# Local attention in float32 parts: the scores' second product from one part of the queries, two heads in the two halves of the array's rows

## The chip, the cores and the metric

The kernel runs on one core of a Trainium2 chip, as one launch. TensorE (PE) multiplies matrices and writes its results to PSUM, which has eight banks of 512 float32 numbers for each of 128 partitions; ScalarE (ACT), VectorE (DVE) and GpSimd (POOL) do the rest; SyncE (SP) issues most of the transfers. The metric is the device time of one execution in microseconds. Three runs of the kernel before took 5764.69, 5766.54 and 5771.52 us; the median is 5766.54 us.

## The reference

The input x is 4 sequences of 2048 tokens with 256 features, in float32. The reference does two things one after the other.

1. A layer norm, then full self-attention with 16 heads of 16 features and a Gaussian prior on the distance added to the scores, an output projection, and the sum with x.
2. A layer norm, then two layers of a local transformer. This is the part that the change touches. Each layer shifts half of the features by one token, projects to queries, keys and values of 8 heads of 64 features, brings queries and keys to unit length, scales and rotates them, and lets each block of 128 queries look at the keys of its own block and of the block before:

```
sim = einsum('bhwid,bhwjd->bhwij', bq, bk)        # 128 queries x 256 keys, 64 features
sim = where((i < j) | (i > j + 128) | (j == -1), -max, sim)
out = einsum('bhwij,bhwjd->bhwid', softmax(sim), bv)
```

After the output projection and the sum comes a second layer norm and a gated unit (256 to 2 x 682, GELU, back to 256).

## The kernel before

The first attention and the preparation of the layers' weights come first (`attention`, up to about 3120 us of the span). Its order is written out by hand. The change does not touch it, but its matmuls are rows to measure with: L859 and L942 are products over 64 rows of the array, written `64*128` in the profile (64 active rows, 128 active columns), two of them side by side; L966 uses the array in quarters of its columns (`128*32`).

The layers are in `local_layers`. A step is one block of 128 tokens of one sequence in one layer: 2 layers x 4 sequences x 16 blocks = 128 steps, and each fourth step also begins the gated unit for four blocks. The pieces of a step are entered in a timetable (`AT`, `put`): 32 slots for a step, with later steps interleaved, so that a step's pieces lie between those of its neighbours. A slot is a place in program order, not a time. From that order a planner makes the order of each engine's instructions at compile time, with its own costs for what is ready when; so a piece can be cut, and others put between its parts.

Products are made accurate by parts: a float32 operand is a high part, rounded to the fast matmul type (fp32r), and a low part, the rest. `dense` (L404) multiplies high by high, high by low and low by high.

For the scores, `attend` does the following:

- `turn` (L1458) transposes queries and keys, two heads to a block of 128 rows: a pair of heads has parity 0 in rows 0 to 63 and parity 1 in rows 64 to 127.
- `high_q` (L1463, ScalarE) and `low_q` (through `low`, L1356, VectorE) fill the queries' tile `lq`. For each parity the high part lies in the head's own 64 rows and the low part in the other 64.
- `high_k` (L1472, ScalarE) and `low_k` (L1356, VectorE) make the keys' two parts in the head's own rows of `lk`, and two transfers (L1478, issued by SyncE) copy both parts to the other 64 rows. The tile has two slots, for the block's own keys and those before.
- `product` (L1494, "sim") then multiplies over all 128 rows: the stacked queries (high over low) with the high keys, twice over, and with the low keys, twice over. That is four terms in two matmuls for each head, 16 matmuls in a step, each 256 columns wide (128 at the first block of a sequence). A pair of heads takes one PSUM bank; the four pairs are at slots 54, 59, 62 and 59.
- `masked` (L1506, VectorE) adds the mask, writes the scores to SBUF and takes their maximum; `weights` (L1520, ScalarE) makes the exponentials; `normalize` (L1531, POOL) divides by the sums.

`gather` of the same step follows: `turn_p` (L1553, "pT") transposes the weights, `copied` (L1564, ScalarE and VectorE by turns) takes them out of PSUM, and `weigh` (L1574, "po") multiplies them with the values, with the array in halves of its columns (`128*64`). The PSUM banks of all of these, of the gated unit's products (`w<-gt,ww`, `w<-ww,mid`) and of the output product `lo` come from one pool of six; the projections `qkv` have two of their own. When a bank's readers are done, another tile can have it.

Of the kernel before, what the change touches and what calls it, by code (L numbers as in the profile page):

```python
# [28 lines left out]
F32 = mybir.dt.float32  # L29
# [8 lines left out]
P = 128  # L38
# [55 lines left out]
    "unit": (22, 15, 41),  # L94
    "turn": (36, 41),
    "parts": (51, 52, 44, 44),
    "sim": (54, 59, 62, 59),
    "masked": (59, 59, 63, 63),
    "weights": (59, 61, 69, 70),
    "normalize": (73, 77, 75, 77),  # L100
# [87 lines left out]
def encoder_kernel(  # L188
# [22 lines left out]
    nc = tc.nc  # L211
# [1072 lines left out]
    def local_layers():  # L1284
        with ExitStack() as es:
# [11 lines left out]
            def psum(name):  # L1297

                banks = pq if name.startswith("qkv_") else pp
                return banks.tile([P, 512], F32, tag="ps", name=name)  # L1300

            qst = [fp.tile([P, 2, 4, P], F32R, tag=f"q{i}", name=f"lq{i}") for i in range(2)]
            kst = fp.tile([P, 2, 2, 2, 4, P], F32R, tag="k", name="lk")
            own = (slice(0, LD), slice(LD, P))
# [16 lines left out]
            def put(at, key, pieces):  # L1324

                assert len(pieces) == len(AT[key]), key
                for slot, piece in zip(AT[key], pieces):
                    tt.put(at + slot, piece)

            def each(f, n):  # L1330
                return [partial(f, i) for i in range(n)]
# [22 lines left out]
            def low(dst, src, h):  # L1354

                nc.vector.tensor_tensor(dst, src, h.bitcast(F32), ALU.subtract)  # L1356
# [88 lines left out]
            def attend(at, l, b, c):  # L1445

                name = f"{l}_{b}_{c}"
                s = state[l, b, c]
                m = {}
                q, slot = qst[c % 2], c % 2  # L1450
                k = kst[:, :, :, slot]

                def turn(i):
                    flat = s["r"][:, i].rearrange("p h d -> p (h d)")
                    ps = psum(f"{'qk'[i]}t_{name}")
                    for pair in range(4):
                        cols = slice(pair * P, (pair + 1) * P)
                        nc.tensor.transpose(ps[:, cols], flat[:, cols], ident)  # L1458
                    m["t", i] = ps.rearrange("p (a t) -> p a t", a=4)

                def high_q():
                    for par in range(2):
                        nc.scalar.copy(q[own[par], par], m["t", 0][own[par]])  # L1463

                def low_q():
                    for par in range(2):
                        r, other = own[par], own[1 - par]
                        low(q[other, par], m["t", 0][r], q[r, par])

                def high_k():  # L1470
                    for par in range(2):
                        nc.scalar.copy(k[own[par], par, 0], m["t", 1][own[par]])  # L1472

                def low_k():
                    for par in range(2):
                        r, other = own[par], own[1 - par]
                        low(k[r, par, 1], m["t", 1][r], k[r, par, 0])
                        nc.sync.dma_start(k[other, par].bitcast(F32), k[r, par].bitcast(F32))  # L1478

                put(at, "turn", each(turn, 2))  # L1480
                put(at, "parts", [high_q, low_q, high_k, low_k])


                width = 2 * P if c else P
                windows = slice(0, 2 if c else 1)
                masks = mask[:, P * (1 - slot) : P * (1 - slot) + width]

                def product(pair):
                    ps = m["ps", pair] = psum(f"sim_{name}_{pair}").rearrange(
                        "p (a t) -> p a t", a=2  # L1490
                    )
                    for par in range(2):
                        for part in range(2):
                            nc.tensor.matmul(  # L1494
                                ps[:, par, :width], q[:, par, pair, :],
                                kst[:, par, part, windows, pair, :], start=part == 0, stop=part == 1,
                            )

                def masked(pair):
                    if pair == 0:  # L1500
                        s["p"] = wp.tile([P, LH, 2 * P], F32, tag="sim", name=f"sim_{name}")
                        for key in ("top", "sums", "inv"):
                            m[key] = small.tile([P, LH], F32, tag=f"l{key}", name=f"{key}_{name}")
                    for par in range(2):
                        h = 2 * pair + par
                        nc.vector.tensor_tensor_reduce(  # L1506
                            s["p"][:, h, :width], m["ps", pair][:, par, :width], masks, 1.0,
                            3.0 * MASKED, ALU.add, ALU.max, m["top"][:, h : h + 1],
                        )
                    if pair % 2:  # L1510
                        hs = slice(2 * pair - 2, 2 * pair + 2)
                        nc.vector.scalar_tensor_tensor(  # L1512
                            m["top"][:, hs], m["top"][:, hs], -1.0, s["rn"][:, hs],
                            ALU.mult, ALU.mult,
                        )

                def weights(pair):
                    for h in (2 * pair, 2 * pair + 1):
                        w = s["p"][:, h, :width]
                        nc.scalar.activation(  # L1520
                            w, w, AF.Exp, bias=m["top"][:, h : h + 1],
                            scale=s["rn"][:, h : h + 1], accum_out=m["sums"][:, h : h + 1],
                        )

                def normalize(pair):
                    if pair % 2 == 0:
                        hs = slice(2 * pair, 2 * pair + 4)
                        nc.vector.reciprocal(m["inv"][:, hs], m["sums"][:, hs])  # L1528
                    hs = slice(2 * pair, 2 * pair + 2)
                    w = s["p"][:, hs, :width]  # L1530
                    nc.gpsimd.tensor_tensor(  # L1531
                        w, w, m["inv"][:, hs].unsqueeze(2).to_broadcast([P, 2, width]), ALU.mult
                    )

                put(at, "sim", each(product, 4))
                put(at, "masked", each(masked, 4))
                put(at, "weights", each(weights, 4))
                put(at, "normalize", each(normalize, 4))
# [244 lines left out]
            for step, (l, b, c) in enumerate(steps):  # L1783
                at = SLOTS * (step + 1)
                if b == 0 and c == 0:
                    if l:
                        tt.put(at + AT["spread"][0], partial(load, l, ("q", "k", "v")))
                    tt.put(at + AT["turn"][0], partial(load, l, ("wo",)))
                    tt.put(at + AT["stats"][0] - 20, partial(load, l, ("w1", "w2")))
                if c % 4 == 0:  # L1790
                    tt.put(max(0, at + FETCH_AT), partial(fetch, l, b, c // 4))
                project(at, l, b, c)
                attend(at, l, b, c)
                gather(at, l, b, c)
                if c % 4 == 0:
                    glu(at, l, b, c // 4)
            tt.run()

    attention()
    local_layers()  # L1800


# [51 lines left out]
```

## Time and profile before

| | before |
|---|---|
| median of three runs | 5766.54 us |
| profiled execution | 5772.22 us, span 5770.4 us |
| mean granted TensorE clock | 0.985 |
| sim matmuls, L1494 | 2048, 339.8 us busy, mean 295 ns |
| their weight loads | 2048, median 189 ns |
| copies of the keys, L1478 | 256 transfers of 256 KB |

Busy time is by instructions, and matmuls are pipelined: a matmul's length in the profile runs from its start to its modelled end, and the next may start long before that. So lengths of matmuls are not added up; the distance from one start to the next says what a matmul costs in a stream. PEld is the loading of weights, which runs beside the matmul before it. A row of the timeline gives the start, the length of the whole group, the engine, the line, the operation, the tiles (output <- inputs), the active rows * columns of the array for PE, the shape, the number of instructions, and in brackets the idle time of the engine just before with what ended it. An idle time of an engine that does not bound the kernel costs nothing.

### The profile page before, as it was taken

The numbers are of one execution on the slowest core, as the hardware profiler recorded it, in microseconds if no ns is written. First come the engines' busy times: TensorE is split into PE (matmuls) and PEld (weight loads), VectorE is DVE, ScalarE is ACT, GpSimd is POOL, SyncE is SP. The second block draws the span as 40 slices with busy tenths as digits, with TensorE's granted clock in tenths as the row PEclk, the third lists the DMA queues.
The fourth block names the chain that finished last, engine by engine and source line by source line (L and its number), as shares of the span: only waits on it lengthen the run. The fifth ranks groups of instructions, "written<-read, shape, count | busy, mean of one in ns | idle before, by whom it ended". The sixth has DMA issues, their size and how long they took to land.

```text
span 5770.4 us, 105485 instructions
## 1 busy us (share of the span) xinstructions
PE 5470.7 (95%) x35544; PEld 3390.2 (59%) x35544; DVE 4836.5 (84%) x13769; ACT 4465.9 (77%) x9400; POOL 2184.3 (38%) x2368
## 2 busy tenths in 40 slices
PE   7999999999999999999997999999999999999998
PEld 4444444444444444444444787888887888888787
DVE  6878999789998789999994888888888788888886
ACT  3879998789988799989996676666666666667665
POOL 3222112221022210010002565666665666666665
PEclk8999999999999999999998999999999999999999
DMA  4444233443234423332213112221223222222211
GB/s 153 140 123 123 79 94 99 124 129 102 84 111 131 130 78 103 87 96 59 67 49 110 51 48 55 51 55 52 55 51 84 83 61 58 60 60 55 67 51 40
DMA packets 337243, 477.30 MB, mean 83 GB/s; under 512 B 67297, under 2 KB 191201, under 8 KB 335169
## 3 DMA queue, kind: packets, MB, share of 16 engines
q1 hardware_dynamic: 323744, 434.36, 27.0%
q0 software_dynamic: 12960, 36.20, 2.2%
q8 instruction: 284, 4.65, 0.3%
q14 instruction: 255, 2.08, 0.1%
HBM read 267.80 MB, written 126.09 MB: 68 GB/s over the span
## 4 chain that ended last, share of the span: by engine, by line
PE 57%; DVE 22%; ACT 8%; POOL 6%; DMA 3%; issue 3%; SPq 0%; POOLq 0%; DVEq 0%; ACTq 0%
PE s L859 16%; PE acc L966 15%; PE s L942 8%; PE w L404 5%; ACT sim L1520 4%; PE sim L1494 3%; DVE s L873 3%; PE qkv L404 3%; POOL rn L373 3%; DVE lk L1356 2%; PE po L1574 2%; DVE sim L1506 2%; DVE hn L1639 2%; DVE tops L871 2%; PE pqk L404 1%
## 5 line engine op out<-in xcount | busy, mean ns | idle before, releaser
L957 ACT ACTIVATE e<-s 128x512 f32<-128x512 f32 x4096 | 2151.1, 612 | 230.9 <-PE s L942 125.4
L859 PE MATMUL s<-k,q 64*128 64x512 f32 x3200 | 1296.2, 466 | 103.0 <-DVE tops L873 69.0
L873 DVE CUSTOM_DVE_ANT_0 s<-s,wide 128x512 f32<-128x512 f32 x1408 | 976.8, 694 | 197.6 <-PE s L859 185.9
L966 PE MATMUL acc<-e,v 128*32 128x512 f32 x8192 | 1100.1, 609 | 0.3 <-ACT rest L980 0.3
L859 PEld LDWEIGHTS s<-k,q 64*128 64x128 f32 x3200 | 531.9, 185 | 550.0 <-ACT more L879 259.1
L942 PE MATMUL s<-q,k 64*128 64x512 f32 x4096 | 833.7, 418 | 5.2 <-issue 2.6
L1520 ACT ACTIVATE sim<-sim,top,rn 128x256 f32<-128x256 f32 (+1 forms) x1024 | 597.2, 586 | 257.5 <-DVE top L1512 256.9
L871 DVE TENSOR_REDUCE tops<-s 128x1 f32<-128x512 f32 x896 | 610.8, 682 | 76.2 <-PE s L859 72.7
L1531 POOL TENSOR_TENSOR sim<-sim,inv 128x512 f32<-128x512 f32 (+1 forms) x512 | 512.8, 1022 | 345.5 <-DVE inv L1528 345.4
L942 PEld LDWEIGHTS s<-q,k 64*128 64x128 f32 x4096 | 542.2, 186 | 130.6 <-ACT e L957 53.4
L883 DVE CUSTOM_DVE_ANT_0 more<-s,more 128x512 f32<-128x512 f32 x896 | 614.3, 686 | 0.3
L859 PEld LDWEIGHTS s<-kd,q 64*128 64x128 f32 x896 | 165.2, 184 | 748.6 <-DVE tops L873 384.3
L879 ACT ACTIVATE more<-s 128x512 f32<-128x512 f32 x896 | 539.7, 602 | 76.3 <-PE s L859 44.4
L404 PE MATMUL w<-gt,ww 128*128 128x512 f32 x2112 | 545.8, 397 | 3.5 <-DVE lk L1356 3.1
L953 DVE TENSOR_TENSOR s<-s,band 128x187 f32<-128x187 f32 (+2 forms) x1408 | 468.7, 354 | 60.5 <-PE s L942 59.8
L859 PE MATMUL s<-kd,q 64*128 64x512 f32 x896 | 447.7, 500 | 0.5 <-DVE tops L871 0.2
L404 PEld LDWEIGHTS w<-gt,ww 128*128 128x128 f32 x2112 | 387.5, 189 | 79.3 <-issue 3.7
L1506 DVE CUSTOM_DVE_ANT_0 sim<-sim,cst 128x256 f32<-128x256 f32 (+1 forms) x1024 | 376.9, 409 | 60.1 <-PE sim L1494 56.8
L1419 POOL TENSOR_TENSOR r<-r,t 128x256 f32<-128x256 f32 x512 | 366.7, 738 | 150.5 <-DVE t L1406 141.0
L997 POOL TENSOR_TENSOR oall<-o,inv 128x256 f32<-128x256 f32 x64 | 39.8, 621 | 983.8 <-DVE inv L996 982.2
L373 POOL TENSOR_TENSOR rn<-ss,nhalf 128x16 f32<-128x16 f32 x128 | 372.7, 2912 | 95.6 <-DVE ss L372 92.7
L1494 PE MATMUL sim<-lk,lq 128*128 128x256 f32 (+1 forms) x2048 | 339.8, 295 | 27.6 <-DVE lq L1356 18.8
(196 smaller groups left out, 9667.6 us busy)
## 6 DMA issues: line engine op xcount, KB each, us to landing
lk<-lk SPq DMA_DIRECT2D x256, 256.0 KB
k<-sm SPq DMA_DIRECT2D x512, 96.0 KB
q<-sm SPq DMA_DIRECT2D x508, 96.0 KB
sm<-part SPq DMA_DIRECT2D x168, 256.0 KB
q<-sm SPq DMA_DIRECT2D x128, 192.0 KB
k<-sm SPq DMA_DIRECT2D x126, 192.0 KB
fg<-f SPq DMA_DIRECT2D x32, 512.0 KB
tb<-td SPq DMA_DIRECT2D x128, 128.0 KB
```

The lines of the kernel that those rows point to most:

```text
L373: nc.gpsimd.tensor_tensor(dst, var, nhalf[:, : var.shape[1]], ALU.pow)
L404: nc.tensor.matmul(ps, a, c, start=first and k == 0 and i == 0, stop=last and k == n - 1 and i == 2,)
L859: nc.tensor.matmul(ps, q1[u // 4 % Q_BUFS][rows, u % 4 * P : (u % 4 + 1) * P], keys, start=True, stop=True,)
L871: nc.vector.tensor_reduce(top, ps, AX.X, ALU.max)
L873: nc.vector.tensor_tensor_reduce(ps, ps, prior, 1.0, LOWEST, ALU.add, ALU.max, top)
L879: nc.scalar.activation(more, pairs.pop((u, 1, half)), AF.Relu)
L883: nc.vector.tensor_tensor_reduce(more, ps, more, 1.0, LOWEST, ALU.add, ALU.max, tops[u // NC][:, chunk(u), 2 * half : 2 * half + 1],)
L942: nc.tensor.matmul(ps, k2[s // 4 % Q_BUFS][rows, kc % 4 * P : (kc % 4 + 1) * P], q2[h % 2][rows, j % 2 * QT : (j % 2 + 1) * QT], start=Tru ...
L957: nc.scalar.activation(e, sums.pop((s, j)), AF.Exp)
L966: nc.tensor.matmul(acc[32 * j : 32 * j + 32, :], vs[b, kc][:, own * VS : own * VS + 32], es_.pop((s, j)), start=kc == 0, stop=kc == NC - 1,)
L1494: nc.tensor.matmul(ps[:, par, :width], q[:, par, pair, :], kst[:, par, part, windows, pair, :], start=part == 0, stop=part == 1,)
L1520: nc.scalar.activation(w, w, AF.Exp, bias=m["top"][:, h : h + 1], scale=s["rn"][:, h : h + 1], accum_out=m["sums"][:, h : h + 1],)
```

## The change

The product with the keys' high parts stays as it is, over all 128 rows. The product with the keys' low parts takes the queries' high parts alone: both lie in the head's own 64 rows, so it is a matmul over 64 rows, and the heads of parity 0 and 1 use the upper and the lower half of the array. The term of low queries by low keys is left out. The low keys need no second copy, so the transfers copy the high keys alone (128 KB instead of 256), and they are issued before `low_k`'s subtractions, after `high_k`.

Two matmuls that run side by side in row halves write to different banks. So the bank is no longer that of a pair of heads but that of a parity: the pieces are two halves of four heads (two pairs), each with two banks, one for each parity, in which the two pairs lie side by side. Within a half come first the four full-array matmuls, then the four over 64 rows. The first matmul into a bank sets `start`, and the last sets `stop`. The halves are at slots 55 and 60. `masked` reads its pair's part of both banks.

```diff
--- before.py
+++ after.py
@@ -94,7 +94,7 @@
     "unit": (22, 15, 41),
     "turn": (36, 41),
     "parts": (51, 52, 44, 44),
-    "sim": (54, 59, 62, 59),
+    "sim": (55, 60),
     "masked": (59, 59, 63, 63),
     "weights": (59, 61, 69, 70),
     "normalize": (73, 77, 75, 77),
@@ -1302,6 +1302,7 @@
 
 
 
+
             qst = [fp.tile([P, 2, 4, P], F32R, tag=f"q{i}", name=f"lq{i}") for i in range(2)]
             kst = fp.tile([P, 2, 2, 2, 4, P], F32R, tag="k", name="lk")
             own = (slice(0, LD), slice(LD, P))
@@ -1474,8 +1475,12 @@
                 def low_k():
                     for par in range(2):
                         r, other = own[par], own[1 - par]
+                        nc.sync.dma_start(
+                            k[other, par, 0].bitcast(F32), k[r, par, 0].bitcast(F32)
+                        )
+                    for par in range(2):
+                        r = own[par]
                         low(k[r, par, 1], m["t", 1][r], k[r, par, 0])
-                        nc.sync.dma_start(k[other, par].bitcast(F32), k[r, par].bitcast(F32))
 
                 put(at, "turn", each(turn, 2))
                 put(at, "parts", [high_q, low_q, high_k, low_k])
@@ -1485,16 +1490,23 @@
                 windows = slice(0, 2 if c else 1)
                 masks = mask[:, P * (1 - slot) : P * (1 - slot) + width]
 
-                def product(pair):
-                    ps = m["ps", pair] = psum(f"sim_{name}_{pair}").rearrange(
-                        "p (a t) -> p a t", a=2
-                    )
-                    for par in range(2):
-                        for part in range(2):
-                            nc.tensor.matmul(
-                                ps[:, par, :width], q[:, par, pair, :],
-                                kst[:, par, part, windows, pair, :], start=part == 0, stop=part == 1,
-                            )
+                def product(half):
+                    banks = [
+                        psum(f"sim_{name}_{half}{par}").rearrange("p (a t) -> p a t", a=2)
+                        for par in range(2)
+                    ]
+                    for i in range(2):
+                        m["ps", 2 * half + i] = [ps[:, i, :width] for ps in banks]
+
+
+                    for part, rows in enumerate(((slice(0, P),) * 2, own)):
+                        for pair in (2 * half, 2 * half + 1):
+                            for par in range(2):
+                                nc.tensor.matmul(
+                                    m["ps", pair][par], q[rows[par], par, pair, :],
+                                    kst[rows[par], par, part, windows, pair, :],
+                                    start=part == pair % 2 == 0, stop=part == pair % 2 == 1,
+                                )
 
                 def masked(pair):
                     if pair == 0:
@@ -1504,7 +1516,7 @@
                     for par in range(2):
                         h = 2 * pair + par
                         nc.vector.tensor_tensor_reduce(
-                            s["p"][:, h, :width], m["ps", pair][:, par, :width], masks, 1.0,
+                            s["p"][:, h, :width], m["ps", pair][par], masks, 1.0,
                             3.0 * MASKED, ALU.add, ALU.max, m["top"][:, h : h + 1],
                         )
                     if pair % 2:
@@ -1532,7 +1544,7 @@
                         w, w, m["inv"][:, hs].unsqueeze(2).to_broadcast([P, 2, width]), ALU.mult
                     )
 
-                put(at, "sim", each(product, 4))
+                put(at, "sim", each(product, 2))
                 put(at, "masked", each(masked, 4))
                 put(at, "weights", each(weights, 4))
                 put(at, "normalize", each(normalize, 4))
```

## The prediction

> **What bounds the kernel now.** I read the page first (shares, slices, groups), then a table of busy time by stretch, then TensorE's timeline around the changed products, then the waits of those products.
>
> ```profile
> PE 5470.7 (95%) x35544; PEld 3390.2 (59%) x35544; DVE 4836.5 (84%) x13769; ACT 4465.9 (77%) x9400; POOL 2184.3 (38%) x2368
> L942 PE MATMUL s<-q,k 64*128 64x512 f32 x4096 | 833.7, 418 | 5.2 <-issue 2.6
> L1494 PE MATMUL sim<-lk,lq 128*128 128x256 f32 (+1 forms) x2048 | 339.8, 295 | 27.6 <-DVE lq L1356 18.8
> ```
>
> The table by stretch, for the two long steady stretches of the layers (columns: length, then busy time of PE, PEld, DVE, ACT, POOL, the granted clock, DMA):
>
> ```profile
> 3200.00:4400.00 1200.00, 1144.80 (x8148) 959.48 (x8148) 1008.08 (x2743) 826.38 (x1934) 740.96 (x674) 1.00 0.21 55
> 4460.00:5600.00 1140.00, 1087.86 (x7759) 915.78 (x7759) 953.55 (x2584) 784.50 (x1832) 744.16 (x667) 1.00 0.23 62
> ```
>
> TensorE is busy 95% in both stretches at full clock, VectorE 84%, so a nanosecond of TensorE there is nearly a nanosecond of the end. The layers run from about 3120 us to the end: 128 steps (2 layers, 4 batches, 16 blocks) of 20.2 us in the steady part. The attention ahead of them is not touched. L1494, the changed line, has 16 matmuls in each step.
>
> TensorE's timeline of one step (start, length, group):
>
> ```profile
> 4514.42 0.74 PE L1494 MATMUL sim<-lk,lq 128*128 128x256 f32 x4
> 4514.99 1.56 PE L404 MATMUL qkv<-wv,ht 128*128 128x512 f32 x6
> 4516.39 1.58 PE L404 MATMUL w<-ww,mid 128*128 128x256 f32 x12
> 4517.81 1.12 PE L1494 MATMUL sim<-lk,lq 128*128 128x256 f32 x8
> 4518.86 1.09 PE L1574 MATMUL po<-pT,lv 128*64 128x128 f32 x16
> 4519.88 1.70 PE L404 MATMUL w<-ww,mid 128*128 128x256 f32 x12
> 4521.42 0.64 PE L1494 MATMUL sim<-lk,lq 128*128 128x256 f32 x4
> 4521.90 1.55 PE L404 MATMUL qkv<-wq,ht 128*128 128x512 f32 x6
> ```
>
> Lengths overlap, so I read from start to start. Twelve matmuls of 256 columns take 4517.81 - 4516.39 = 1.42 us, 0.118 each; six of 512 take 1.40, 0.23 each. Now the changes of the array's shape. The 8 sim matmuls ahead of po (array in column halves, 128*64) take 1.05 us where 8 x 0.118 = 0.94: **leaving** a shape costs 0.09 to 0.11. The 12 w matmuls that follow po take 1.54, not 1.42: **entering** one costs 0.12, for the first matmul's weights have nothing to hide behind. Sim after po, in another step, shows it again: 0.58 for 4, where 4521.42 to 4521.90 is 0.48.
>
> ```profile
> 4500.12 0.74 PE L1494 MATMUL sim<-lk,lq 128*128 128x256 f32 x4
> 4500.70 1.53 PE L404 MATMUL qkv<-wq,ht 128*128 128x512 f32 x6
> ```
>
> Row halves (64*128), which the change uses, appear beside full-array work only early in the attention:
>
> ```profile
> 58.63 1.68 PE L404 MATMUL pv<-aw,xT 128*128 128x256 f32 x12
> 60.24 0.50 PE L859 MATMUL s<-kd,q 64*128 64x512 f32 x1
> ...
> 61.55 0.49 PE L859 MATMUL s<-k,q 64*128 64x512 f32 x1 [0.58 <-ACT more L879]
> 61.97 1.68 PE L404 MATMUL pv<-aw,xT 128*128 128x256 f32 x12
> ```
>
> The 12 full-array matmuls between them take 1.61 us: 1.42 + 0.10 + 0.09. And one lone half-row matmul takes 0.42 until the full array starts, against 0.23 in a stream: 0.19 for entering and leaving. So a change to or from row halves costs what one to column halves does, about **0.20 us** (0.19 to 0.22).
>
> **What the change removes.** Of the 16 matmuls of a step, the 8 with the keys' low parts now take 64 rows each, two side by side. The nearest row for that is L942: 418 ns each, yet 833.7 busy us over 4096, 0.204 each, half of the length, so pairs do overlap. Eight slots of 0.118 become four: **-0.47 us a step** (at block 0 of each sequence, 8 steps with 128 columns, -0.24 to -0.44).
>
> **What it adds.** Each group of 8 goes full array, row halves, and on. Half 0 needs a change in and a change out. Half 1 needs one in; its way out falls together with the change that sim (or w) makes before po already. So 3 more changes x 0.20 = **+0.60 us a step**; the return from po to full-array work is there before and after. Net +0.13 us in the ordinary step. In about one step of four (30) the first-layer product `w<-gt` of the gated unit stood between the sim matmuls and po, and there the change out is paid again: +0.33. Sum: 90 x 0.13 + 30 x 0.33 + 8 x 0.25 = 11.7 + 9.9 + 2.0 = **+24 us**. With 0.19 and 0.22 for a change instead: +19 and +32.
>
> The Trainium skill, "TensorE: Matmul & The Clock Gate", Part 3, gives the span of packed tiles as one matmul's length plus about 4 ns for each further tile and prices no change of shape; "TensorEngine Tiling (Array Packing)", Key Properties, says that changing the mode drains the array and gives no price. By the first alone, an estimate, the pairs would gain about 59 us. The rows above price the drain, so I go by the rows.
>
> **Cuts.** The layers' order is the planner's, which mixes pieces by its own costs; in this trace's timeline sim runs are cut at times (2 matmuls, then another product, then the rest). A cut inside a row-half block costs two more changes, 0.40. I estimate 15 cuts in 256 blocks: +6 us (bounds 0 and 20).
>
> **What moves.** SyncE's two key copies now wait for ScalarE's rounding alone, not for VectorE's subtractions (L1356, 0.69 us each), and carry half the bytes. SP's queue behind them (table loads, fetches, the shift copies) is released earlier by as much; those waits have slack and I cost them at nothing. If that cover were gone, they would still be earlier, not later. VectorE's low parts are the same two instructions. What the products wait for:
>
> ```profile
>   DVE lq L1356: 46.1, 57
>   DMA lk<-lk: 15.7, 20
> ```
>
> The copy's 15.7 us (PE's and PEld's idle together) shrinks: I take **-10** (bounds -15.7 and 0). The 46.1 for the queries' low parts: in the steady part one step of four stands some 0.9 us there, because the filling work had already been used up:
>
> ```profile
> 3412.98 0.96 PE L1494 MATMUL sim<-lk,lq 128*128 128x256 f32 x4 [0.65 <-DVE lq L1356]
> ```
>
> The full-array product still comes first and still needs those parts, so I leave it: 0 (bounds -46 and 0).
>
> **Banks.** Before, a pair of heads took one bank; now a half takes two at once and keeps them until both its pairs are masked. The total is the same, the pressure is not: six banks, of which two hold the second product's sums during nearly two steps of four. TensorE already waits for banks:
>
> ```profile
> PE pT L1553 <- DVE lk L1356: 31.2, 65, 1.5
> PE pT L1553 <- DVE lq L1356: 14.4, 28, 0.5
> ```
>
> A half that finds no second bank waits for one copy out, 0.68 us (L1564 on VectorE). Bounds: 0 and 64 x 0.68 = +44; less than nothing is possible only through the planner. I take +3, near the low end, for the planner can put other matmuls there. The masking (L1506) reads the same columns, 0.42 us each.
>
> **Sum.** 24 + 6 - 10 + 0 + 3 = +23 us. The profiled execution took 5772.2 us (span 5770.4), 5.7 above the median of the runs; against the median, 5766.5 + 23 = 5789.5, so **5790**.
>
> **Rivals.**
> 1. *Faster by a vanished wait.* Half 0 is placed a little later, behind the values' product (6 x 0.23 = 1.4 us), which covers both waits in front of sim, 61.8 us in all. Then 24 + 6 + 3 - 62 = -29: 5738. It ends faster once more than some 45 of the 62 us go. For: in the ordinary step the values' product does come right after sim. Against: where the 0.9 us are lost, another product had already been taken ahead (qkv of wk stood just before sim).
> 2. *Slower by banks.* +44 instead of +3: 5831. For: the waits of pT. Against: in the step shown, ScalarE had copied two of the four transposes out (4511.95 and 4514.27 + 0.58) before or just as sim began, so two banks were free.
> 3. *The change of shape is free*, -59 - 10: about 5698. Against: 0.42 against 0.23 above.
> 4. *The halves don't run side by side* (the change doesn't do what it says): +0.47 more in a step, +60: 5850. Against: L942's busy time.
>
> **How the numbers follow.** Forecast 0.52, its own range 5772 to 5812 (switch price, cuts and copy at their bounds); rival 1 0.20; rival 2 0.14; rival 3 0.03; rival 4 0.03; 0.08 for a planner's order that evens it out. A difference within 0.2% (11.5 us, about what a measurement of this kernel can tell from none) gets those 0.08, 0.04 of the forecast's low end and 0.03 of rival 1: 0.15. Faster: 0.17 + 0.03 = 0.20. Slower: the rest, 0.65. The range 5740 to 5834 leaves out rivals 3 and 4, and the outer parts of 1 and 2: about 0.2.
>
> **What would show it.** Right: sim rows in two forms, 128*128 and 64*128, 8 matmuls a step of each; in each half about 0.21 us from the last full-array start to the first pair, 0.22 to 0.24 from the first pair to the second, 0.21 to what follows; a group of 8 takes 0.99 to 1.05 us where 0.94 was; steps 0.1 to 0.3 us longer; copies of 128 KB. Wrong: a start-to-start of 0.12 across a change of shape (rival 3), sim without waits and steps under 20.2 us (rival 1), new idle time ahead of sim ended by VectorE's copies or masks (rival 2), pairs 0.12 apart within (rival 4). The likeliest way to be wrong is the planner's order: two or three different cuts a step outweigh the net.

## The result, and the profile after

| | before | after |
|---|---|---|
| median of four runs | 5768.48 us (5764.69 to 5771.52) | 5806.38 us (5802.54 to 5815.97) |
| profiled execution | 5772.22 us, span 5770.4 us | 5806.55 us, span 5804.7 us |
| mean granted TensorE clock | 0.985 | 0.984 |

After is slower: the ratio is 1.0067, with a 95% interval of 1.0055 to 1.008, some 38 us. The forecast was +23.

The page of after: the engines' busy time, the group of the changed products, and the keys' copies:

```profile
PE 5504.8 (95%) x35544; PEld 3379.2 (58%) x35544; DVE 4803.1 (83%) x13769; ACT 4488.3 (77%) x9400; POOL 2194.8 (38%) x2368
L1505 PE MATMUL sim<-lk,lq 64*128 64x256 f32 (+3 forms) x2048 | 332.3, 316 | 39.6 <-DVE res L1781 33.0
lk<-lk SPq DMA_DIRECT2D x256, 128.0 KB
```

The change does what it says: half rows (64\*128) appear, the copies are half as large, and each engine has as many instructions as before. TensorE is busy 95% as before, which tells nothing of the 38 us. What is new is at the end of the second line: the scores' products now wait for `res`, the gated unit's last sums. Before they waited for the queries' low parts (`lq`).

The table by stretch, for the first of the two stretches shown of before (length, then busy time of PE, PEld, DVE, ACT, POOL, the granted clock, DMA):

```profile
3200.00:4400.00 1200.00, 1137.62 (x7991) 936.38 (x7990) 970.70 (x2692) 815.38 (x1883) 732.20 (x660) 1.00 0.16 42
```

TensorE got through 7991 matmuls in those 1200 us, where it was 8148: 1.9% fewer, at the same clock (1.00), the same share of busy time (95%) and with less for the DMA engines to do (0.16, before 0.21). The two stretches do not hold exactly the same steps; the count by groups below does.

What TensorE's idle time before the changed line waited for (us, times):

```profile
  DVE res L1781: 75.5, 60
  DVE lq L1357: 14.2, 35
```

This counts PE and PEld together, as the two lines of before did. The copy's wait (15.7 before) is gone from the list, the wait for `lq` fell from 46.1 to 14.2, and 75.5 for `res` is new. By TensorE's own count, `PE sim <- DVE res` is 33.0 us.

**One ordinary step, and one that is cut.** The timeline of TensorE, an ordinary step:

```profile
3290.64 1.07 PE L1505 MATMUL sim<-lk,lq 128*128 128x256 f32 x8
3291.64 1.09 PE L1586 MATMUL po<-pT,lv 128*64 128x128 f32 x16
```

From start to start 8 sim matmuls take 1.00 us; two such halves take 2.00, where 16 matmuls in a stream would take 16 x 0.118 = 1.89. But before was no plain stream either: the step that the forecast shows took 0.57 + 1.05 + 0.48 = 2.10 us, for there too sim paid for the changes of shape around po. Within the group, four full-array starts stand 0.120 apart, the first pair of half rows comes 0.209 later, its two heads 0.003 apart, the second pair 0.219 after that, and po 0.206 later still. All these distances were forecast (0.21, 0.22 to 0.24, 0.21, a group of 0.99 to 1.05).

One step of every four looks like this instead:

```profile
3325.20 0.48 PE L404 MATMUL qkv<-wk,ht 128*128 128x512 f32 x1
3325.55 1.79 PE L1505 MATMUL sim<-lk,lq 128*128 128x256 f32 x8
3327.28 0.50 PE L404 MATMUL qkv<-wq,ht 128*128 128x512 f32 x1
3327.61 0.83 PE L1505 MATMUL sim<-lk,lq 128*128 128x256 f32 x4
3328.37 0.96 PE L404 MATMUL qkv<-wq,ht 128*128 128x512 f32 x3
3329.17 0.83 PE L1505 MATMUL sim<-lk,lq 128*128 128x256 f32 x4
3329.93 1.09 PE L1586 MATMUL po<-pT,lv 128*64 128x128 f32 x16
```

The groups of four are half of a half: the planner took the matmuls of one parity, two full and two half rows, before those of the other. The two half-row matmuls then lie in the same rows and did not run side by side: their starts are 0.222 to 0.224 apart instead of 0.003. (The trace does not name the rows of a matmul. That these two share them follows from the kernel's loops; in e1 below, where the program order is kept, no such pair is left.) Start to start the 16 sim matmuls take 1.73 + 0.76 + 0.76 = 3.25 us, against 2.00 in the ordinary step. Some 30 steps are cut this way. That 30 x 1.25 = 38 us equals the whole loss is chance, for the same step of a group was a long one in before too: the one whose sim starts at 3412.98 us took 0.79 + 1.04 + 0.58 = 2.41. So sim grew by 0.84 us in the cut step, some 25 us in all.

**The new wait**, in the same view:

```profile
3307.66 0.28 PE L1505 MATMUL sim<-lk,lq 128*128 128x256 f32 x1
3308.86 2.16 PE L1505 MATMUL sim<-lk,lq 128*128 128x256 f32 x15 [0.92 <-DVE res L1781]
```

One sim matmul goes, then TensorE stands 0.92 us. The first bank of half 0 was free, the second still held the gated unit's sums, which VectorE had not yet added to `res`. It is the second bank that a half takes at once. Such a wait stands in each group of four steps, about 1.1 us in the ordinary ones; whether it lengthens the group is seen only when the other waits are counted too.

**Where the time went, by groups of four steps.** The GELU of the gated unit comes once in four steps, 32 times; the time from one to the next is a group.

| | before | after | difference in all |
|---|---|---|---|
| first GELU, in the span | 3273.0 us | 3264.7 us | -8.3 |
| 23 ordinary groups | 80.0 to 81.4 us | 82.0 to 82.1 (one 83.5) | +28 |
| 6 groups with a first block of a sequence | 80.1 to 80.7 | 83.3 to 85.5 | +22 |
| the group at the border of the layers | 92.3 | 83.7 | -8.6 |
| the last | 44.3 | 45.1 | +0.8 |
| sum | | | +34 |

The span differs by 34.3. In three of the six groups with a first block after had a lower granted clock, 0.96 to 0.98; they took 84.1, 84.2 and 85.5 us, the other three, at 1.00, took 83.3. So some 4 of the 22 us go with the clock. To see what an ordinary group is made of, I went through the starts of its 558 matmuls and split the time in three: what they take in a stream (0.118 for 256 columns, 0.23 for 512, a pair of half rows counted once), what the starts are further apart than that without idle time (changes of shape, mostly), and idle time.

| us in a group | stream | changes of shape, and the like | number of changes | idle | sum |
|---|---|---|---|---|---|
| before | 71.7 | 4.9 | 16 | 4.3 | 80.9 |
| after | 69.8 | 8.0 | 33 | 4.2 | 82.0 |

The pairs gave 1.9 us and the changes took 3.1. This counts all 16 pairs of a group once, though the four of the cut step do not run side by side; counted as they ran, the pairs gave 1.4 and the changes took 2.6. The idle time is the same: waits for sim's banks and for `lv` rose (`qkv`: 0.3 to 1.1), waits ahead of the transposes pT fell (2.7 to 2.0). In the groups with a first block, sim stood idle 2.5 us (1.9 of them for `res`) where it had stood 0 to 1.1.

### The profile page after: what moved, and what is told of

It is laid out like the page before. It is cut to its first block, busy times and chain, and to the rows that moved or that the text cites. A ratio compares the mean times of both kernels' runs of the same rounds, so it can differ in the third digit from the quotient of the medians.

```text
span 5804.7 us, 105688 instructions
## 1 busy us (share of the span) xinstructions
PE 5504.8 (95%) x35544; PEld 3379.2 (58%) x35544; DVE 4803.1 (83%) x13769; ACT 4488.3 (77%) x9400; POOL 2194.8 (38%) x2368
## 4 chain that ended last, share of the span: by engine, by line
PE 63%; DVE 19%; ACT 6%; POOL 5%; issue 3%; DMA 2%; SPq 1%; POOLq 0%; DVEq 0%; ACTq 0%
PE s L859 15%; PE acc L966 15%; PE s L942 8%; PE w L404 6%; PE qkv L404 5%; PE sim L1505 3%; POOL rn L373 3%; PE po L1586 3%; DVE s L873 3%; ACT sim L1532 3%; DVE lk L1357 2%; PE pT L1565 2%; DVE tops L871 2%; PE pqk L404 1%; DVE sim L1518 1%
## 5 line engine op out<-in xcount | busy, mean ns | idle before, releaser
L1505 PE MATMUL sim<-lk,lq 64*128 64x256 f32 (+3 forms) x2048 | 332.3, 316 | 39.6 <-DVE res L1781 33.0
```

## The experiments

My theory after the result was that the cut of the halves by parity makes most of the loss, beside pairs and changes at their forecast prices. The first rival: the second bank, taken at once, and what it waits for. The second: the planner's order of everything else, which it made anew. All times are medians, each against before on the same chip.

**Tie the order, drop the half rows, drop the product.** `e1_pinned` ties each sim matmul of a half to the place behind the one before it, so that no half is cut by parity (mm is the matmul):

```diff
-                                nc.tensor.matmul(
+                                mm = nc.tensor.matmul(
...
+                                if (part, pair % 2, par) != (0, 0, 0):
+                                    tc.keep_in_program_order(mm)
```

> The changed kernel, with each sim matmul of a half tied behind the one before it, so that the planner can't take the heads of one parity first (in one step of four it runs two full, two half-row, and these two lie in the same half of the array, 0.22 us apart). Theory A (the planner's order undoes the pairing in that step): four blocks of 0.86 us become two of about 1.1, 1.2 us in each of 30 groups of four steps, 37 us back, less up to 0.7 us a group for waiting until both parities' low queries are there: 5770 to 5790 us. Theory B (the wait of sim for a bank is what costs): nothing changes, 5800 to 5810.

`e2_full_rows` keeps the halves, banks and slots of after, but multiplies the low keys over all 128 rows again (their second copy comes back, as transfers of their own, after the subtractions):

```diff
                         low(k[r, par, 1], m["t", 1][r], k[r, par, 0])
+                        nc.sync.dma_start(
+                            k[other, par, 1].bitcast(F32), k[r, par, 1].bitcast(F32)
+                        )
...
-                    for part, rows in enumerate(((slice(0, P),) * 2, own)):
+                    for part, rows in enumerate(((slice(0, P),) * 2,) * 2):
```

> The changed kernel's banks, slots and early copy of the high keys, but the product with the low keys over all 128 rows again (the low parts are copied too, by two transfers more after the subtractions). No change of the array's shape is left in the scores. Theory A (shape changes and half-row matmuls in the same half): the loss of the steady groups goes, about 1.1 to 1.2 us in 32 groups, 5765 to 5775 us. Theory B (banks and slots): it stays, 5795 to 5810.

`e3_high_keys_only_after` and `e4_high_keys_only_before` take the second product away from after and from before (the flags for the first and the last matmul of a bank are set to match, not shown):

```diff
-                    for part, rows in enumerate(((slice(0, P),) * 2, own)):
+                    for part, rows in enumerate(((slice(0, P),) * 2,)):
```

```diff
-                        for part in range(2):
+                        for part in range(1):
```

> The changed kernel without the product with the low keys, which is left out of the computation: 8 full-array matmuls a step in the changed banks and slots, no row halves. Theory A: as long as the next run within 10 us, for banks and slots cost little; about 5650 us. Theory B: 30 to 40 us longer than the next run.

> The kernel before without the product with the low keys, which is left out of the computation: 8 of the 16 sim matmuls of a step, in the banks and slots of before. If TensorE bounds the layers throughout, 8 x 0.118 us x 128 steps = 121 us less: 5648 us. If other engines hold the step as well, less than half of that: over 5700.

| before: 5769.53 us | us | ratio, 95% |
|---|---|---|
| e1_pinned | 5744.93 | 0.9955 (0.9941 to 0.997) |
| e2_full_rows | 5766.21 | 0.9993 (0.9983 to 1.0002) |
| e3_high_keys_only_after | 5712.22 | 0.9894 (0.9878 to 0.9911) |
| e4_high_keys_only_before | 5747.09 | 0.9958 (0.9943 to 0.9973) |

e1 takes 61 us from after, more than the 37 of its theory A, and is 25 us faster than before, with the same half rows, banks and copies. Its timeline in the step that was cut:

```profile
3331.10 1.83 PE L1505 MATMUL sim<-lk,lq 128*128 128x256 f32 x9
3332.77 0.39 PE L404 MATMUL qkv<-wq,ht 128*128 128x512 f32 x1
```

Nine matmuls of sim go in one run, the first half and one more; the runs of one parity are gone, and every pair of half rows starts within 0.006 us. The 16 take 2.54 us from start to start, instead of 3.25. An ordinary group takes 79.9 us, with 30 changes instead of 33 (7.0 us for 8.0) and 3.0 us of idle time for 4.2: pT waits 0.55 us in a group instead of 2.0. So the cut holds for about 1.0 x 31 = 31 us of the 61, and the rest goes with waits that another order no longer has. The wait for `res` stayed:

```profile
PE sim L1505 <- DVE res L1783: 32.8, 29, 1.9
```

So the second bank's wait is there in full, and the kernel is 25 us faster than before all the same.

e4 was the surprise. It takes 1024 matmuls of 0.118 us, 121 us, off an engine that is busy 95% of the time, and gains 22, less than half, as the second case of its expectation had it. Its waits of TensorE over the whole span (us, times, longest):

```profile
PE pT L1553 <- DVE lk L1356: 55.5, 66, 1.8
PE sim L1494 <- DMA lk<-lk: 37.4, 60, 1.1
PE kt L1458 <- DVE r L1438: 34.6, 26, 2.8
```

In before the same three had been 32.0, 4.9 and 4.0 us, by TensorE's own count as here. Take work off TensorE, and the copy, the transposes' banks and the normalization `r` come due at once. TensorE was almost never idle, and still not what bound the steps alone. Its granted clock was a little lower in e4 too, 0.982 for 0.985 in the profiled executions; 0.003 of the span is 17 us at most, so this does not change the reading.

e3 fits neither theory: it was to be level with e4 or 30 to 40 us longer, and it is 35 us shorter, with as many matmuls. Its copies are early, and in its trace sim waits 0.6 us for them instead of 37.4. That was a first sign of what e10 shows below.

**Which part of the change costs, which gains.** `e5_full_rows_pinned` is e2 with the tie of e1; `e6_before_pinned` is before, with the four matmuls of each pair of heads tied in the same way:

```diff
-                            nc.tensor.matmul(
+                            mm = nc.tensor.matmul(
...
+                            if (par, part) != (0, 0):
+                                tc.keep_in_program_order(mm)
```

`e7_more_shape_changes` is e1 with the two loops exchanged, so that each pair of heads changes the shape: the same matmuls, 4 changes more in a step:

```diff
-                    for part, rows in enumerate(((slice(0, P),) * 2, own)):
-                        for pair in (2 * half, 2 * half + 1):
+                    for pair in (2 * half, 2 * half + 1):
+                        for part, rows in enumerate(((slice(0, P),) * 2, own)):
```

`e8_one_block` makes one piece of the two halves: eight full-array matmuls, then four pairs of half rows, with four banks at once, all tied in order as in e1 (the banks' loop is not shown):

```diff
-    "sim": (55, 60),
+    "sim": (57,),
...
-                        for pair in (2 * half, 2 * half + 1):
+                        for pair in range(4):
```

> Full rows for both products in the changed kernel's banks and slots, with the sim matmuls of a half tied in order as in the pinned kernel (5744.9 us). It differs from that one by the row halves alone. Theory A (row halves pay less than their shape changes cost): in the pinned ledger a group of four steps saves 1.87 us of streaming and pays 2.1 for 14 changes more, so full rows would be 0.3 us a group faster, 5735 us; anything from 5725 to 5745 fits. Theory C (the pairs side by side are a gain once they are kept): slower than 5744.9 by 10 us or more.

> The kernel before with the four sim matmuls of a pair tied in order, and nothing else. If the gain of the pinned kernel comes from keeping the planner from cutting sim, whatever the shape, this one gains too, 10 to 25 us (5745 to 5760). If it comes from the changed banks, slots and copies, it stays at 5768.

> The pinned kernel with each pair of heads finished before the next: two full, two half-row (side by side), two full, two half-row in each half. The same matmuls, four changes of shape more in a step. By the rows of before a change costs 0.20 us: 0.78 us a step, 100 us, 5845 us, if every one is felt at the end; 5800 to 5845 if the gaps hide part. If a change of shape is free, 5745.

> All four pairs in one piece (slot 57), four banks at once: eight full-array matmuls, then eight over 64 rows, tied in order. Two changes of shape fewer in a step than the pinned kernel. Theory A: 0.39 us a step, 50 us, down to 5695. Theory B (banks): four banks at once make TensorE wait for copies and sums, 0.7 to 2 us a step, which eats it: 5745 to 5850.

| before: 5766.51 us | us | ratio, 95% |
|---|---|---|
| e5_full_rows_pinned | 5737.2 | 0.9946 (0.9931 to 0.9961) |
| e6_before_pinned | 5769.62 | 1.0006 (0.9996 to 1.0015) |
| e7_more_shape_changes | 5860.5 | 1.0163 (1.0148 to 1.0178) |
| e8_one_block | 5720.72 | 0.992 (0.9903 to 0.9936) |

e7 prices the change of shape, but not as simply as its time suggests. It is 5860.5 - 5744.9 = 116 us over e1, more than the 100 that its expectation allowed, 0.226 us for each of the 128 x 4 changes. The first of the two stretches, in e7 and then in e1:

```profile
3200.00:4400.00 1200.00, 1163.09 (x7882) 938.50 (x7879) 952.17 (x2626) 805.17 (x1863) 720.25 (x653) 0.98 0.14 38
3200.00:4400.00 1200.00, 1155.08 (x8224) 950.32 (x8226) 991.65 (x2772) 836.02 (x1945) 750.29 (x678) 1.00 0.16 43
```

The granted clock of e7 was 0.98 here and 0.97 in the second stretch, that of e1 1.00 in both. The groups of e7 that had the full clock throughout took 82.4 us, against 79.9 in e1: 2.5 us for 16 changes more, **0.16 each**. In these groups TensorE's starts lie 2.7 us further apart without idle time, so what the changes cost TensorE is felt nearly in full. Over 32 groups that is 80 of the 116 us; the rest goes with the lower clock. Why the clock was lower is not shown.

e6 says that the tie itself is worth nothing in before (+3, the interval holds 1), where no pieces of a shape can be torn apart. e5 gives 29 us over e2, though it has no half rows at all: the tie helps the layout in halves by its order, and here the cut of half rows can't be the reason. Where there are half rows to tear apart, the tie gives 61 - 29 = 32 us more, as the groups of e1 said. And e5 stands 8 us under e1 (the intervals of the two ratios overlap): with both in order, half rows in two halves, with the copy that they save, gain nothing that could be told.

In one block it is otherwise. The step in e8:

```profile
3285.01 0.76 PE L1504 MATMUL sim<-lk,lq 128*128 128x256 f32 x5
3285.60 0.28 PE L404 MATMUL w<-ww,mid 128*128 128x256 f32 x1
3285.72 1.19 PE L1504 MATMUL sim<-lk,lq 128*128 128x256 f32 x11
3286.84 1.58 PE L404 MATMUL w<-ww,mid 128*128 128x256 f32 x11
```

From start to start sim takes 0.59 + 1.12 = 1.71 us; in e9 below, with full rows, the same step takes 1.91. There is one change in and one out for four pairs, whose later ones follow after some 0.115 us. e8 falls between its theories (5695, or 5745 and more), and differs from e5 in slot and banks as well; e9 takes the half rows alone.

**The copy alone, the block alone, and the sums.** `e9_one_block_full_rows` is e8 with full rows for both products (the two edits of e2). `e10_early_copy_before` is before with nothing but the copies changed: the high keys are copied before the subtractions, the low keys after them, the bytes are the same:

```diff
+                        nc.sync.dma_start(
+                            k[other, par, 0].bitcast(F32), k[r, par, 0].bitcast(F32)
+                        )
+                    for par in range(2):
+                        r, other = own[par], own[1 - par]
                         low(k[r, par, 1], m["t", 1][r], k[r, par, 0])
-                        nc.sync.dma_start(k[other, par].bitcast(F32), k[r, par].bitcast(F32))
+                        nc.sync.dma_start(
+                            k[other, par, 1].bitcast(F32), k[r, par, 1].bitcast(F32)
+                        )
```

`e11_pinned_sums_earlier` is e1, and `e12_one_block_sums_earlier` is e8, with the gated unit's last sums entered earlier, so that the bank they hold comes free before sim asks for it:

```diff
-    "after": (352, 359),
+    "after": (339, 340),
```

> The one-block kernel (5720.7 us) with the product with the low keys over all 128 rows and the low parts copied too: no change of shape in the scores. With one block a step, the row halves save 0.47 us and pay one change in (0.20 to 0.22; the change out falls together with the one before po in three steps of four): theory A expects full rows to be 0.2 us a step slower, 25 to 30 us, 5745 to 5752. If row halves never pay, it is 5720 or less.

> The kernel before, with the copy alone changed: the high keys are copied right after the rounding, the low keys after the subtractions, four transfers of 128 KB a step in place of two of 256. My forecast gave the earlier and smaller copy 10 us: 5757 us. If the copy was hidden but for the ends of the layers, 5762 to 5770.

> The pinned kernel (5744.9 us) with the gated unit's last sums, which free the two banks that sim waits for, put 13 and 19 slots earlier in program order (339 and 340 in place of 352 and 359). If that wait (33 us of TensorE's idle time before sim, ended by VectorE's res) holds the end, 15 to 33 us less: 5712 to 5730. If another wait takes its place, 5740 to 5750.

> The one-block kernel (5720.7 us) with the same earlier sums. Its own trace shows no wait of sim for these sums, so nothing is to be had: 5712 to 5728. A gain like the pinned kernel's would mean that the banks hold this one too.

| before: 5765.41 us | us | ratio, 95% |
|---|---|---|
| e9_one_block_full_rows | 5744.23 | 0.9958 (0.9943 to 0.9973) |
| e10_early_copy_before | 5722.24 | 0.992 (0.9905 to 0.9934) |
| e11_pinned_sums_earlier | 5745.71 | 0.9955 (0.994 to 0.997) |
| e12_one_block_sums_earlier | 5716.52 | 0.991 (0.9893 to 0.9926) |

e9 against e8: half rows in one block, with the copy that they save, gain 23.5 us, and the intervals are apart. In the profiled executions it is 17: an ordinary group takes 79.6 us in e8 and 80.1 or 80.2 in e9, 0.5 to 0.6 us, and the border of the layers 82.6 and 86.1. That is less than the four times 0.20 us that sim itself saves; a group of e8 has 23 changes of shape instead of 16, and not all of their cost falls on sim (the first two `w` matmuls behind the block shown start 0.222 apart, not 0.118).

e10 is the largest single gain of the study, 43 us, from the copies alone; its expectation had 10 at most. The sim group and its idle time:

```profile
L1501 PE MATMUL sim<-lk,lq 128*128 128x256 f32 (+1 forms) x2048 | 339.3, 297 | 18.4 <-DVE lq L1356 10.3
```

The products are as long as before (339.8); the idle time ahead of them fell from 27.6 to 18.4, so nine of the 43 us are there. By groups: the first GELU comes 17.9 us earlier (3255.1), the border of the layers takes 85.2 instead of 92.3, and most of the others 78.4 to 80.5 instead of 80.1 to 81.2. At the border before had stood for the copy:

```profile
4449.74 1.58 PE L1494 MATMUL sim<-lk,lq 128*128 128x256 f32 x6 [3.81 <-DMA lk<-lk]
```

Not all of the 17.9 can be laid to the copies. The attention ended 6 us earlier in e10, and over all kept traces its end lies between 3076 and 3086 us, with early copies and late; and from 3120 us to the first GELU the granted clock was 0.94 in e10 and 0.90 in before. Still, most of the gain is in places where no wait of before carried the copy's name; by what path the steps between got shorter is not shown.

e11 moved nothing, and tells nothing of the wait: the planner moved the second of the two sums and left the first where it was. VectorE's timeline in e1 shows what the first stands behind:

```profile
3313.03 0.17 DVE L1438 TENSOR_SCALAR rn<-rn 128x8 f32<-128x8 f32 x1 [2.12 <-POOL rn L373]
3313.11 0.68 DVE L1439 TENSOR_TENSOR r<-r,rn 128x512 f32<-128x512 f32 x1
3313.71 0.68 DVE L1783 TENSOR_TENSOR res<-res,w 128x512 f32<-128x512 f32 x1
```

VectorE stood 2.12 us for a norm that POOL makes (`rn`), and the sum came after. In e11 this order is the same, and `PE sim <- DVE res` is 31.9 us for 31.9 in e1 over the same stretch (3200 to 5600). What the kernel would gain without that wait was not measured. e12 is the fastest of all, 9 per thousand under before; against e8 (0.992) the intervals overlap, so the earlier sums are not shown to help there.

**The steps from before to after**, by these runs:

| from | to | us |
|---|---|---|
| before | copies alone earlier (e10) | -43 |
| e10 | halves, two banks at once, other slots (e2) | +44 |
| e2 | half rows for the low keys, half the copies (after) | +40 |
| sum | | +41 (measured +38) |

The before of the four sets of runs lies between 5765 and 5770 us, so steps across sets are good to some 4 us. The middle step has the banks, the slots and the planner's new order in it; the first two were not separated. That much of it is order is shown by e5: the tie alone gives back 29 of the 44. In the last step it is the same: with both kernels tied (e5 and e1) the 40 are 8. The steps need not have the same size when taken in another sequence.

## Why the prediction was right or wrong

The sign and the range held: slower, 5806 within 5740 to 5834, +38 for +23, inside the forecast's own range of 5772 to 5812. That the sum came near the result is luck in good part: two terms that were each wrong by some 30 to 40 us, the copy and the banks, have opposite signs.

1. *"A nanosecond of TensorE there is nearly a nanosecond of the end."* Wrong as a rule for gains. e4 took 121 us away and gained 22; e10 took nothing from TensorE's work and gained 43. It held for a loss: 16 more changes of shape in a group of e7, at full clock, put TensorE's starts 2.7 us further apart, and the group took 2.5 us more. What was added to the full engine was passed on to the end; what was taken from it went to the next things that were late, and in e4 three were waiting just behind.
2. *Pairs -0.47 a step.* Right in three steps of four, where two heads start 0.003 apart. In the cut step they do not, so a group gained 1.4 us instead of 1.9.
3. *Three more changes at 0.20.* The price was about right: on the way into row halves the first pair is 0.09 us later than in a stream and the second 0.10 (0.209 and 0.219 for 0.12), as the rows of before had said; over whole groups a change cost 0.16 (e7 at full clock). The sum of pairs and changes, +24, was too high: with the order tied in both, half rows cost 8 us (e1 against e5), and the intervals overlap. The Trainium skill, "TensorEngine Tiling (Array Packing)", Key Properties, says that a change of tiling mode drains the array; the runs show a cost of 0.16 to 0.2 us for a change, but not that it is a drain.
4. *Cuts +6.* The term that failed in the sense of the forecast's last sentence ("the planner's order"). I had 15 cuts of 0.40; there are some 30 cut steps, and they cost some 1.0 us each, 31 us (the groups of after and e1) or 32 (what the tie gives in after beyond what it gives in e2). Number and price were both too low, for one kind of cut was not thought of: by parity, which doesn't only add changes but takes away the side-by-side run for which the change was made. Tying the order returned 61 us, so about half of it by this.
5. *Copy -10, bounds -15.7 and 0.* Wrong by a factor of four, and outside its bounds: e10 measures -43. I read the copy's worth from the idle time that bore its name. In the traces of before and after it can be seen at the border of the layers (-8.6; in e10 -7.1), where TensorE had stood 3.81 us for it. The earlier start (-8.3; in e10 -17.9) may be the copy's too, but the attention's end alone moves by such amounts between the runs. e10's copies have all the bytes of before, so it prices the earlier start of the transfers, not their half size.
6. *Wait for the queries' low parts, 0.* The wait did shrink, from 46.1 to 14.2; the wait for `res` came in its place (75.5). The rival "faster by a vanished wait" had the first half right.
7. *Banks +3, bounds 0 and +44.* The step to halves, banks and slots cost +44, by chance just the upper bound, in the planner's order; +15 with the order tied (e5 5737 against e10 5722). A new wait for a second bank did appear, 33.0 us by TensorE's count, but for the gated unit's sums and not for the copies out of pT, which the forecast had looked at. How much of the 44 is that wait stays open.
8. *Rivals 3 and 4* (change of shape free; no side by side) are refuted by the start-to-start times in after. Rival 4 came true in the cut steps only.

## What to carry to other kernels

Row halves need a block that is long enough: at 0.16 to 0.2 us for each change of shape, four pairs of 256 columns in one block gained 17 to 24 us here, the same four in two blocks gained nothing that could be told, and the planner must be kept from tearing a block apart by halves. Look at the granted clock before pricing a change by the time of the whole kernel: in e7 a third of the difference went with it. Idle time under the name of a transfer is not what an earlier transfer is worth: the order of four copies was the best single edit here, found only when it was tried alone. When an edit changes products, banks, slots and copies at once, price them one at a time; here +38 was made of -43, +44 and +40.

## What the runs showed of the hardware

- Two half-row matmuls of after start 0.003 us apart when they lie in different halves of the rows, and 0.222 to 0.224 apart when they follow one another in the same half, behind a change of shape (256 columns take 0.118 in a full-array stream).
- Behind a change between the full array and row halves the second start is late: in the cut step the two full-array matmuls after half rows start 0.223 apart, and in an ordinary step the second pair of half rows comes 0.219 after the first. From the third pair on, in one block, it is some 0.115. So the 0.222 above is no more than this, and what a longer run in one half would take is not shown.
- A change of shape costs 0.16 us in whole groups at full clock (e7 against e1, 16 changes more). With these changes the granted clock of the two stretches fell from 1.00 to 0.98 and 0.97, though TensorE was no less busy (97% of both stretches in e7, 96 and 97% in e1).
- The planner's order matters as much as the work: the tie of a few matmuls to their order, with the same instructions, moved the kernel by 61 us in after, 29 in e2 and nothing that can be told in before.
